# Four layers of graph network on one core: background tiles loaded on another queue, attention ranges in ascending order, entry counts in bf16 pairs

## The chip, the cores and the metric

The kernel runs on one core of a Trainium2 chip, in one launch. The metric is the device time of one execution in microseconds (us); lower is better. "PE" is TensorE, "DVE" VectorE, "ACT" ScalarE, "POOL" GpSimd, and "SP" SyncE, which only issues DMAs here. ACT and POOL issue DMAs too.

## The reference

Inputs are `x` (2708 x 512) and a dense matrix `adj` (2708 x 2708, float32, about 1% of its entries not zero). Each layer ends in a layernorm of (its input plus its output). The constants and unused inputs are left out here:

```python
deg = max(sum(adj != 0, axis=-1), 1)
# layer 0
inc = adj + normalised(adj > 0);  x = layernorm(x + (inc @ x) / sum(inc, -1))
# layer 1
type_sum = adj @ x
attn_a = sigmoid([type_sum, x] @ Wa.T);  attn_b = sigmoid([type_sum, x] @ Wb.T)
h = x @ W_sa;  s_left = h @ a_sa[0, :512];  s_right = h @ a_sa[0, 512:]
e = where(adj != 0, exp(-leaky_relu(s_left[:, None] + s_right[None, :])), 0)
x_a = (e / (sum(e, 1) + 1e-5)) @ h
x_b = adj @ (x @ W_gcnb) + b_gcnb
x = layernorm(x + sigmoid(attn_a * x_a + attn_b * x_b))
# layer 2: three hops
out = x @ W[0];  p = x;  for i in 1..3: p = adj @ p; out += p @ W[i]
x = layernorm(x + out)
# layer 3
a_norm = dinv * (adj + I) * dinv, dinv = rsqrt(deg)
x = layernorm(x + relu((a_norm @ x + x) @ W3 + b3))
```

So `adj`, or a matrix of its shape, is multiplied by a 2708 x 512 matrix seven times, and the count of entries of each row (`deg`) is needed in layer 3 only.

## The kernel before

The host passes `adj` transposed (`adjT`). Rows and columns are cut in two halves of `NH` = 1354, a half has `KT` = 11 tiles (ten of 128 and one of 74; the short rows of both halves are packed into the tiles `r` and `r32`). Every product is done with fewer block products than a plain 2 x 2 blocking, so that DVE makes sums and differences of quarters of `adj` ahead of PE: `sweep` does seven products in place of eight on tiles of `adj` of 128 x (256 to 384) columns; `sweep2` does the same at two levels.

Work is listed by hand. `at(pos, fn)` puts a function into a list with a position, the list is sorted by position and run; each function records its instructions. Each engine keeps its own order of instructions and runs on when its semaphores allow. One unit of position is one block product of one range of columns, so a range takes 7 units. The stages:

- `S[0]`: layer 0, four ranges. `S[1]`: the type sum of layer 1 for the columns 1024 to 1353 of each half only (`RANGES_A`), on which its result (`x_b` times its gate) goes to `XB` in memory; `comb` there also saves the sums of quarters to the memory `SD` (`As` in the profile).
- `S[2]`: attention. Scores `e` are made by ACT (Prelu and Exp, L1142, L1143), DVE masks them by `adj` (L1144), and the sweep multiplies them with `x`. Its ranges are `RANGES_S` = (1024, 330), (768, 256), (384, 384), (0, 384), each with its loads `a<-in_adjT` on SP from one unit ahead of its start. A row of scores `row<-SR` (L1151) is fetched before each.
- Beside `S[2]` runs a *background* pass over the other columns, 0 to 767, in 22 rounds of 1.13 units. A round loads one tile 128 x 512 of each quarter into `bk` (`back_load`, L1058; four tiles with one buffer each), counts its entries (`back_tally`: ACT Sign L1071 and Square L1072, DVE add L1074), makes four sums in place (`back_sums`, DVE L1094) and stores them to `SD` from POOL (L1095). The last round of each half of the columns takes the short rows (`back_rest_load`, L1065) and `back_end` adds the counts up on PE (`ds`, L1102).
- `SB`: the second part of layer 1's type sum, by `sweep2`, on those stored sums. `S[3]` to `S[5]`: the hops. `S[6]`: layer 3.

At the end of each attention range `done2` multiplies with `W_sa` (`dense`, `ps_d`, L611). For the 330 range, which it calls `whole`, everything of layer 1 is then known: it reads `XB` and `X1` on SP, adds (L1201), takes the sigmoid on ACT (L1204), adds `x` (L1167), normalises (statistics L560 to L564 on DVE, the power on POOL L565, L567 on DVE, ACT L570), stores `X2`, transposes it on PE (L600) and stores `X2T`. The other ranges store `x_a` to `XB` (`xa`), and the second part finishes them. `y0_last` reads `X2T` back and multiplies those tiles by a weight of layer 2.

In the type-sum stage `extra1` counts the entries of its columns: one DVE instruction (L976, L979) for each tile of `adj` adds "not zero" into a float32 tile `deg` for each half; `end` adds each up on PE (L993) and `rows` sends the result out by a transpose. Scores of all tiles of `x` are made there as well (L908 on DVE); `score_rows` sends them out by `to_rows`: a PE transpose (L925), an ACT copy (L927) and a store on POOL. The tiles `ld`, `vy`, `sg`, `dg`, `xa`, `y` come from one pool of six buffers (`nat`). In the profile, `acca`, `accu`, `accc`, `accd` are the accumulators of a sweep, `P1c`, `U2`, `W`, `C` its results in SBUF (added up in L524), `run` and `rs` the row sums of `e` (L771, L784), `ps_n` the transposes of L594.

Of the kernel before, what the change touches and what calls it, by code (L numbers as in the profile page):

```python
# [22 lines left out]
BF = mybir.dt.bfloat16  # L23
AF = mybir.ActivationFunctionType
ALU = mybir.AluOpType
P = 128
EPS = 1e-5
NH = 1354
KT = 11
RANGES = [(0, 384), (384, 384), (768, 256), (1024, 330)]  # L30
# [9 lines left out]


RANGES_A = [(1024, 330)]
RANGES_S = [(1024, 330), (768, 256), (384, 384), (0, 384)]
RANGES_B = [(512, 256), (0, 256)]
RANGES2 = [(676, 339), (0, 338)]
EARLY2 = 6
# [4 lines left out]
KW = 2 * K2  # L51
# [3 lines left out]
KR = NH - KW * P  # L55
KA = 2 * KR - 32
# [6 lines left out]
def wt(k):  # L63
    return min(P, NH - k * P) if k < KT else P
# [8 lines left out]
def gnn_kernel(ctx: ExitStack, tc: tile.TileContext, x, adjT, w_sa, a_sa, w_gcn, b_gcn, wab, bab, w_hop, w_out,  # L73
               b_out, out):
    nc = tc.nc
    N, D = x.shape
# [7 lines left out]
    pool = ctx.enter_context(tc.tile_pool(name="pool", bufs=1))  # L84
# [6 lines left out]
    ones_bf = const.tile([P, P], BF, name="ones_bf")  # L91
    nc.vector.memset(ones_bf, 1.0)
    ones_f = const.tile([P, 1], F32, name="ones_f")
# [55 lines left out]
    def move(queue, dst, src):  # L149

        m = dst.shape[0]
        c = m - m % 16 if m > 16 else m
        queue.dma_start(out=dst[:c], in_=src[:c])
        if c < m:
            queue.dma_start(out=dst[c:m], in_=src[c:m])
# [4 lines left out]
    def tmp(nm):  # L160
        return pool.tile([P, 384], F32, name=nm, tag="tmp", bufs=NTMP)
# [18 lines left out]
    def at(pos, fn, hold=False):  # L180

        def go():
            n = len(nc.cur_bb.bb.instructions)
            fn()
            held.update(range(n, len(nc.cur_bb.bb.instructions)))

        events.append((pos, len(events), go if hold else fn))
# [89 lines left out]
    def rows_over(q, t, src):  # L277

        move(q, t[:KR], src[0])
        move(q, t[KR:KA], src[1][: KA - KR])  # L280
# [407 lines left out]
    S = [0.0, 28.0, 35.0, 91.0, 119.0, 147.0, 175.0]  # L688
    SB = 63.0
# [6 lines left out]
    def tiles_of(R0, n):  # L696
        return list(range(R0 // P, (R0 + n + P - 1) // P))
# [189 lines left out]
    deg = {}  # L887
# [42 lines left out]
    def score_rows(R0, h, ts):  # L930
        q = slice(h * KT + ts[0], h * KT + ts[-1] + 1)
        to_rows(s_left[:, q], len(ts), SROW[R0, h])
# [10 lines left out]
    def get_x1(t):  # L943
        got1[t] = fetch(X1[t])

    i = 0
    for R0, n in RANGES:
        full = R0 == RANGES_A[0][0]
        for h in (1, 0):
            ts = tiles_of(R0, n)  # L950
            for k in ts:
                p = S[1] + 0.55 + 0.21 * i
                at(p, lambda t=h * KT + k: get_x1(t))
                at(p + 0.25, lambda t=h * KT + k, w=wt(k), js=range(4 if full else 2): score(t, w, got1, js))
                i += 1
            at(p + 0.26, lambda a=(h * KT + ts[0], len(ts), False): scores_end(*a))
            if full:
                at(p + 0.26, lambda a=(h * KT + ts[0], len(ts), True): scores_end(*a))
            at(p + 0.3, lambda R0=R0, h=h, ts=ts: score_rows(R0, h, ts))
    at(p + 0.27, scores_over)  # L960
    for i, (h, k) in enumerate((h, k) for g in (4, 0) for h in (0, 1) for k in range(g, g + 4)):
        p = S[2] + 1.6 + 1.3 * i
# [5 lines left out]
    def extra1(pb, r, R0, n, A):  # L968
        ts = tiles_of(R0, n)

        def tally(h, key, w=P):

            a = A[(r,) + key]
            if (R0, h) not in deg:
                deg[R0, h] = d = tmp("deg")
                nc.vector.tensor_scalar(d[:w, :n], a[:w, :n], 0.0, None, ALU.not_equal)  # L976
            else:
                d = deg[R0, h]
                nc.vector.scalar_tensor_tensor(d[:w, :n], a[:w, :n], 0.0, d[:w, :n], ALU.not_equal, ALU.add)  # L979

        for ij, p in (("11", -0.6), ("21", 0.05), ("22", 1.05), ("12", 3.6)):
            for k in range(KW):
                at(pb + p + 0.8 * k / KT, lambda ij=ij, k=k: tally(int(ij[0]) - 1, (ij, k)))
        for h, p in ((1, 2.0), (0, 4.5)):
            at(pb + p, lambda h=h: tally(h, ("r", h), KA))
            at(pb + p, lambda h=h: tally(h, ("r32", h), 32))

        def end(h):
            d = deg.pop((R0, h))
            ps = bank("ds", [P, 4])  # L990
            for i, q in enumerate(ts):
                wq = wt(q)
                nc.tensor.matmul(ps[:wq, i : i + 1], d[:, q * P - R0 : q * P - R0 + wq], ones_f, start=True, stop=True)  # L993
            for i, q in enumerate(ts):
                wq = wt(q)
                o = rdeg[:wq, h * KT + q : h * KT + q + 1]
                nc.vector.tensor_scalar(o, ps[:wq, i : i + 1], 1.0, None, ALU.max)
                nc.vector.tensor_scalar(diag[:wq, h, q : q + 1], o, 1.0, None, ALU.add)
                nc.vector.reciprocal(o, o)

        def rows(h):
            to_rows(rdeg[:, h * KT + ts[0] : h * KT + ts[-1] + 1], len(ts),
                    DROW[h][0, ts[0] * P : (ts[-1] + 1) * P].rearrange("(k i) -> k i", i=P))

        at(pb + 2.6, lambda: end(1))
        at(pb + 3.2, lambda: rows(1))
        at(pb + 5.2, lambda: end(0))
        at(pb + 5.8, lambda: rows(0))

    def done1(p0, dp, last, R0, n, h, C, tiles):  # L1010
        Z = {}
# [42 lines left out]
    def back_load(i0, k):  # L1054
        back["t"] = ts = back_tiles()
        for t, (hi, hj) in zip(ts, QUARTERS):
            j0, c0 = hj * NH + k * P, hi * NH + i0
            nc.sync.dma_start(out=t, in_=adjT[j0 : j0 + P, c0 : c0 + D])  # L1058

    def back_rest_load(i0):  # L1060
        back["t"] = ts = back_tiles()
        for h in range(2):
            a = adjT[:, h * NH + i0 : h * NH + i0 + D]
            rows_over(nc.sync, ts[h], (a[NH - KR : NH], a[2 * NH - KR :]))
            nc.sync.dma_start(out=ts[2 + h][:32], in_=a[2 * NH - 32 :])  # L1065

    def tally(pair, w):

# [21 lines left out]
    def back_sums(i0, k):  # L1090
        a11, a21, a22, a12 = back["t"]
        for m, o, a, b, op in (("s1", a22, a21, a22, ALU.add), ("s3", a21, a11, a21, ALU.subtract),
                               ("s2", a11, a22, a11, ALU.subtract), ("s4", a12, a12, a11, ALU.subtract)):
            nc.vector.tensor_tensor(o, a, b, op)  # L1094
            nc.gpsimd.dma_start(out=SD[m][k * P : (k + 1) * P, i0 : i0 + D], in_=o)  # L1095

    def back_end(i0):
        d = back.pop("d")
        ps = bank("ds", [P, 8])
        for h in range(2):  # L1100
            for i in range(4):
                nc.tensor.matmul(ps[:, 4 * h + i : 4 * h + i + 1], d[:, h, i * P : (i + 1) * P], ones_bf[:, 0:1], start=True,  # L1102
                                 stop=True)
        for h in range(2):
            q = slice(h * KT + i0 // P, h * KT + i0 // P + 4)
            o = rdeg[:, q]
            nc.vector.tensor_scalar(o, ps[:, 4 * h : 4 * h + 4], 1.0, None, ALU.max)
            nc.vector.tensor_scalar(diag[:, h, i0 // P : i0 // P + 4], o, 1.0, None, ALU.add)
            nc.vector.reciprocal(o, o)
# [5 lines left out]
    p = S[2] + 1.3  # L1115
    for i0, _ in RANGES_B:
        at(p, back_start)
        for k in range(KW):
            at(p, lambda i0=i0, k=k: back_load(i0, k))
            at(p + 0.4, back_tally)  # L1120
            at(p + 0.55, lambda i0=i0, k=k: back_sums(i0, k))
            p += 1.13
        at(p, lambda i0=i0: back_rest_load(i0))
        at(p + 0.4, back_rest_tally)
        at(p + 0.6, lambda i0=i0: back_end(i0))
        at(p + 0.9, lambda i0=i0: back_rows(i0, 0))
        at(p + 0.95, lambda i0=i0: back_rows(i0, 1))
        p += 1.13
# [93 lines left out]
            at(q + 0.1, d)  # L1222
            at(q + 0.32 + 0.6 * dp * i, e)

    sweep(S[2], RANGES_S, prep=prep2, extra=extra2, done=done2, sums=True)


    def split(h, r0, w):
# [249 lines left out]
    def y0_last(t, w, r0):  # L1478
        g, (i0, m) = next((g, r) for g, r in enumerate(RANGES2) if r[0] <= r0 and r0 + w <= r[0] + 2 * r[1])
        xT = pool.tile([P, DC, P], F32, name="xT", tag="xT", bufs=2)  # L1480
        nc.sync.dma_start(out=xT[:, :, :w], in_=X2T[g, t // KT][:, r0 - i0 : r0 - i0 + w].rearrange("(c p) i -> p c i", p=P))
        y0_rows(xT, w, t)

    for i, (h, k) in enumerate((h, k) for h in (1, 0) for k in tiles_of(*RANGES_A[0])):
        at(SB + 0.9 + 0.8 * i, lambda t=h * KT + k, w=wt(k), r0=k * P: y0_last(t, w, r0))

    def doneB(p0, dp, g, i0, n, h, cc, tiles):
        Z = {}
# [63 lines left out]
    for i in range(4):  # L1552
        for g, p in enumerate((SB + 19.3 + 1.8 * i, S[3] + 6.6 + 1.3 * i)):
            a = ({}, g, i // 2, i % 2)
# [173 lines left out]
    last, done = {}, {}  # L1728
    for n, i in enumerate(list(nc.cur_bb.bb.instructions)):
        p = last if n < 3 * strict else done if n in held else {}  # L1730
# [44 lines left out]
```

## Time and profile before

| what | us |
|---|---|
| median of 3 runs | 2939.11 |
| lowest and highest run | 2936.87, 2945.16 |
| profiled execution | 2952.44 |
| its span | 2950.4 |
| PE busy | 2845.3 (96%) |
| DVE busy | 2297.5 (78%) |
| ACT busy | 635.4 (22%) |
| POOL busy | 597.5 (20%) |

The profile is of one execution on the chip: span is the time from its first to its last instruction. "Busy" leaves out register, semaphore and DMA-issuing instructions. A line such as `PE ps_d L611 <- DVE P1c L524: 11.8, 2, 8.3` in the list of waits says that PE, at line 611, waited for DVE's line 524: 11.8 us in all, twice, 8.3 the longest. In the timeline the bracket after an instruction is the idle time of its engine before it and what ended it. "PEclk" or granted clock is the TensorE clock that was granted, 1 being full speed. The stages in the trace: layer 0 to 437 us, the type sum to 565, attention to 690, 770, 890 and 1010 (its four ranges), the second part to 1370, the hops to 1760, 2140 and 2520, layer 3 to the end.

### The profile page before, as it was taken

To read this page: it belongs to the slowest core of one execution; us is meant where nothing else is said; L and a number is where in the kernel's file an instruction comes from. 1 tells how busy PE (TensorE), PEld (TensorE's weight loads), DVE (VectorE), ACT (ScalarE), POOL (GpSimd) and SP (SyncE) were. 2 spreads that over 40 slices of the span, in tenths; PEclk is the share of its full clock that TensorE was granted. 3 is DMA by queue.
4 is the path that set the end of the run, shared out by engine and by line. 5 is a ranking of instruction groups with operands and counts; after the bars stand their busy time and mean duration, and the time that the engine had idled before them with its cause. 6 is when DMAs were issued, how large, how long until landed. Compare 5 with 4: busy or idle time off the path is not lost.

```text
span 2950.4 us, 38888 instructions
## 1 busy us (share of the span) xinstructions
PE 2845.3 (96%) x11165; PEld 1919.7 (65%) x11165; DVE 2297.5 (78%) x5912; ACT 635.4 (22%) x1255; POOL 597.5 (20%) x1075
## 2 busy tenths in 40 slices
PE   7999998998999999999999999999999999999998
PEld 5655665566756577777666666666666666656664
DVE  6898797686785636667589877988778877899986
ACT  3554200566656410211200000000000100100001
POOL 0133223212211100123202215012240221501102
PEclk9999998999999999999999999999999999999999
DMA  7666466466666445578668668566685566854542
GB/s 224 182 207 182 137 197 198 138 214 182 223 211 193 133 133 154 169 208 249 212 204 245 202 182 271 158 191 211 194 255 165 169 202 185 242 155 142 179 141 78
DMA packets 410238, 554.41 MB, mean 188 GB/s; under 512 B 68656, under 2 KB 350460, under 8 KB 410024
## 3 DMA queue, kind: packets, MB, share of 16 engines
q1 hardware_dynamic: 343360, 413.52, 48.2%
q0 software_dynamic: 48928, 126.64, 12.9%
q10 hardware_dynamic: 17736, 11.76, 1.4%
q8 instruction: 89, 1.46, 0.2%
q14 instruction: 125, 1.02, 0.1%
HBM read 468.02 MB, written 83.65 MB: 187 GB/s over the span
## 4 chain that ended last, share of the span: by engine, by line
PE 70%; DVE 11%; issue 7%; DMA 6%; POOL 3%; SPq 1%; ACT 1%; POOLq 0%; DVEq 0%; ACTq 0%
PE accd L1355 13%; PE accu L1355 12%; PE accc L1355 12%; PE acca L1355 6%; PE ps_d L611 6%; PE accd L463 4%; PE accc L463 3%; PE accu L463 3%; PE accr L1426 3%; PE acca L463 2%; DVE z L1300 1%; PE accr L1430 1%; POOL rstd L565 1%; DMA ld<-X 1%; DVE vy L908 1%
## 5 line engine op out<-in xcount | busy, mean ns | idle before, releaser
L1300 DVE TENSOR_TENSOR z<-z 128x339 f32<-128x339 f32 (+2 forms) x1176 | 537.7, 488 | 25.4 <-PE accu L1355 14.3
L1373 ACT COPY q<-accu 128x339 f32<-128x339 f32 (+2 forms) x105 | 41.6, 429 | 1062.0 <-PE accu L1355 911.9
L1355 PE MATMUL accc<-s,t 128*128 128x339 f32 (+2 forms) x784 | 233.7, 439 | 0.2 <-DVE s L1300 0.2
L1355 PE MATMUL accu<-z,t 128*128 128x339 f32 (+2 forms) x784 | 227.7, 436 | 4.3 <-DVE z L1300 3.0
L1355 PE MATMUL accd<-z,t 128*128 128x339 f32 (+2 forms) x784 | 227.4, 436 | 1.8 <-DVE q L1437 1.4
L1355 PE MATMUL accc<-z,t 128*128 128x339 f32 (+2 forms) x784 | 226.8, 436 | 0.5 <-ACT q L1373 0.5
L565 POOL TENSOR_TENSOR rstd<-rstd,neg_half 128x1 f32<-128x1 f32 (+3 forms) x91 | 60.6, 666 | 720.7 <-DVE rstd L564 466.9
L1355 PEld LDWEIGHTS accu<-z,t 128*128 128x128 f32 x784 | 148.3, 190 | 71.2 <-DVE z L1300 6.2
L1355 PEld LDWEIGHTS accc<-s,t 128*128 128x128 f32 x784 | 146.8, 190 | 71.1 <-issue 10.7
L1355 PEld LDWEIGHTS accd<-z,t 128*128 128x128 f32 x784 | 148.1, 190 | 65.9 <-DVE q L1437 2.3
L1355 PEld LDWEIGHTS accc<-z,t 128*128 128x128 f32 x784 | 148.2, 190 | 64.8 <-ACT q L1373 1.0
L1300 DVE TENSOR_TENSOR s<-z 128x339 f32<-128x339 f32 (+2 forms) x392 | 177.4, 487 | 9.8 <-PE accd L463 3.8
L1379 DVE TENSOR_TENSOR q<-q,accd 128x338 f32<-128x338 f32 (+2 forms) x140 | 67.7, 484 | 146.1 <-PE accd L1355 145.8
L1574 POOL DMA_DIRECT2D Y<-y x192 | 104.6, 552 | 322.4 <-DVE y L1569 289.8
L408 DVE TENSOR_TENSOR a<-a,a 128x384 f32<-128x384 f32 (+2 forms) x240 | 117.8, 511 | 0.7
L1144 DVE SCALAR_TENSOR_TENSOR a<-a,e 128x384 f32<-128x384 f32 (+2 forms) x160 | 77.5, 505 | 51.0 <-ACT e L1143 44.7
L1142 ACT ACTIVATE e<-row,s_right 128x384 f32<-128x384 f32 (+4 forms) x176 | 94.5, 566 | 33.6 <-DMA row<-SR 16.8
L570 ACT ACTIVATE ld<-ld,rstd 128x512 f32<-128x512 f32 (+3 forms) x45 | 36.5, 813 | 256.9 <-DVE rstd L567 94.1
L1095 POOL DMA_DIRECT2D As<-bk x80 | 43.5, 543 | 223.5 <-DVE bk L1094 212.2
L1437 DVE TENSOR_TENSOR q<-q,accr 128x338 f32<-128x338 f32 (+2 forms) x160 | 69.0, 483 | 20.7 <-PE accr L1430 20.5
L1379 DVE TENSOR_TENSOR q<-q,accu 128x338 f32<-128x338 f32 (+2 forms) x175 | 79.0, 483 | 3.8 <-ACT q L1373 2.6
L775 DVE SCALAR_TENSOR_TENSOR s<-a,row 128x384 f32<-128x384 f32 (+2 forms) x152 | 75.0, 506 | 6.0 <-ACT row L760 6.0
(694 smaller groups left out, 5884.1 us busy)
## 6 DMA issues: line engine op xcount, KB each, us to landing
z<-As SPq DMA_DIRECT2D x320, 169.5 KB
z<-As SPq DMA_DIRECT2D x320, 169.0 KB
z<-in_adjT SPq DMA_DIRECT2D x240, 169.5 KB
z<-in_adjT SPq DMA_DIRECT2D x240, 169.0 KB
a<-in_adjT SPq DMA_DIRECT2D x160, 192.0 KB
bk<-in_adjT SPq DMA_DIRECT2D x80, 256.0 KB
As<-bk POOLq DMA_DIRECT2D x80, 256.0 KB, 3.5
z<-As SPq DMA_DIRECT2D x160, 128.0 KB
```

Of the source, the lines that this page charges most:

```text
L408: nc.vector.tensor_tensor(A[r, dst, k][:, :n], A[r, a, k][:, :n], A[r, b, k][:, :n], op)
L463: nc.tensor.matmul(B[home, c][:, :n], X[STAT[p], k][:, c * P : (c + 1) * P], A[r, MOV[p], k][:, :n], start=bool(start and k == k0), stop=k ...
L565: nc.gpsimd.tensor_tensor(rstd[:w, 1:2], rstd[:w, 0:1], neg_half[:w], ALU.pow)
L611: nc.tensor.matmul(o, lhs(c), r, start=c == 0 and n == 0, stop=c == DC - 1, skip_group_check=True)
L775: nc.vector.scalar_tensor_tensor(t[:w, :n], a[:w, :n], 0.0, row[R0, h][:w, :n], ALU.is_gt, ALU.mult)
L1142: nc.scalar.activation(e[:w, :n], row[R0, h][:w, :n], AF.Prelu, bias=s_right[:w, t : t + 1], alpha=0.01)
L1144: nc.vector.scalar_tensor_tensor(a[:w, :n], a[:w, :n], 0.0, e[:w, :n], ALU.not_equal, ALU.mult)
L1300: nc.vector.tensor_tensor(d[:, :n], Z[x + (k,)][:, :n], Z[y + (k,)][:, :n], op)
L1355: nc.tensor.matmul(B[home][:, :n], stat(v, k), a[:, :n], start=bool(start and k == 0), stop=k == nk - 1, skip_group_check=True)
L1379: nc.vector.tensor_tensor(d[:, :n], s_[:, :n], B[home][:, :n], ALU.add)
L1426: nc.tensor.matmul(ps[r][:, :n], XA[:KA, c * P : (c + 1) * P], R[h, s][:KA, :n], start=True, stop=False, skip_group_check=True)
L1574: nc.gpsimd.dma_start(out=rows[:, :, f * P : (f + 1) * P], in_=o[32 * f : 32 * (f + 1), : m * P].rearrange("p (b d) -> p b d", d=P))
```

## The change

Three things are changed, with the positions that go with them. The background tiles are loaded by GpSimd's queue, and their tally, their sums and the end of the count are listed .15 to .25 units later. The attention ranges go in ascending order, so that the 330 range with its full epilogue is the last; `y0_last` is listed later. In the type-sum stage entries are counted as in the background: ACT's Sign and Square of two tiles into one bf16 tile, and one DVE add for both halves; both ends of the count come at 5.2 units. Besides, the rows of scores are sent out .5 units later.

```diff
@@ -40,7 +40,6 @@
 
 
 RANGES_A = [(1024, 330)]
-RANGES_S = [(1024, 330), (768, 256), (384, 384), (0, 384)]
 RANGES_B = [(512, 256), (0, 256)]
 RANGES2 = [(676, 339), (0, 338)]
 EARLY2 = 6
@@ -956,7 +955,7 @@
             at(p + 0.26, lambda a=(h * KT + ts[0], len(ts), False): scores_end(*a))
             if full:
                 at(p + 0.26, lambda a=(h * KT + ts[0], len(ts), True): scores_end(*a))
-            at(p + 0.3, lambda R0=R0, h=h, ts=ts: score_rows(R0, h, ts))
+            at(p + 0.8, lambda R0=R0, h=h, ts=ts: score_rows(R0, h, ts))
     at(p + 0.27, scores_over)
     for i, (h, k) in enumerate((h, k) for g in (4, 0) for h in (0, 1) for k in range(g, g + 4)):
         p = S[2] + 1.6 + 1.3 * i
@@ -968,29 +967,31 @@
     def extra1(pb, r, R0, n, A):
         ts = tiles_of(R0, n)
 
-        def tally(h, key, w=P):
-
-            a = A[(r,) + key]
-            if (R0, h) not in deg:
-                deg[R0, h] = d = tmp("deg")
-                nc.vector.tensor_scalar(d[:w, :n], a[:w, :n], 0.0, None, ALU.not_equal)
+        def pair(keys, w=P):
+            m = pool.tile([P, 2, D], BF, name="sg", tag="nat", bufs=6)
+            for h, key in enumerate(keys):
+                nc.scalar.activation(m[:w, h, :n], A[(r,) + key][:w, :n], AF.Sign)
+            nc.scalar.activation(m[:w, :, :n], m[:w, :, :n], AF.Square)
+            if R0 not in deg:
+                deg[R0] = d = pool.tile([P, 2, D], BF, name="dg", tag="nat", bufs=6)
+                nc.vector.tensor_copy(d[:w, :, :n], m[:w, :, :n])
             else:
-                d = deg[R0, h]
-                nc.vector.scalar_tensor_tensor(d[:w, :n], a[:w, :n], 0.0, d[:w, :n], ALU.not_equal, ALU.add)
-
-        for ij, p in (("11", -0.6), ("21", 0.05), ("22", 1.05), ("12", 3.6)):
-            for k in range(KW):
-                at(pb + p + 0.8 * k / KT, lambda ij=ij, k=k: tally(int(ij[0]) - 1, (ij, k)))
-        for h, p in ((1, 2.0), (0, 4.5)):
-            at(pb + p, lambda h=h: tally(h, ("r", h), KA))
-            at(pb + p, lambda h=h: tally(h, ("r32", h), 32))
+                d = deg[R0]
+                nc.vector.tensor_tensor(d[:w, :, :n], d[:w, :, :n], m[:w, :, :n], ALU.add)
+
+        for k in range(KW):
+            at(pb + 0.1 + 0.8 * k / KT, lambda k=k: pair((("11", k), ("21", k))))
+            at(pb + 3.9 + 0.8 * k / KT, lambda k=k: pair((("12", k), ("22", k))))
+        for key, w in (("r", KA), ("r32", 32)):
+            at(pb + 4.8, lambda key=key, w=w: pair(((key, 0), (key, 1)), w))
 
         def end(h):
-            d = deg.pop((R0, h))
+            d = deg[R0]
             ps = bank("ds", [P, 4])
             for i, q in enumerate(ts):
                 wq = wt(q)
-                nc.tensor.matmul(ps[:wq, i : i + 1], d[:, q * P - R0 : q * P - R0 + wq], ones_f, start=True, stop=True)
+                nc.tensor.matmul(ps[:wq, i : i + 1], d[:, h, q * P - R0 : q * P - R0 + wq], ones_bf[:, 0:1], start=True,
+                                 stop=True)
             for i, q in enumerate(ts):
                 wq = wt(q)
                 o = rdeg[:wq, h * KT + q : h * KT + q + 1]
@@ -1002,10 +1003,10 @@
             to_rows(rdeg[:, h * KT + ts[0] : h * KT + ts[-1] + 1], len(ts),
                     DROW[h][0, ts[0] * P : (ts[-1] + 1) * P].rearrange("(k i) -> k i", i=P))
 
-        at(pb + 2.6, lambda: end(1))
-        at(pb + 3.2, lambda: rows(1))
+        at(pb + 5.2, lambda: end(1))
+        at(pb + 5.9, lambda: rows(1))
         at(pb + 5.2, lambda: end(0))
-        at(pb + 5.8, lambda: rows(0))
+        at(pb + 5.9, lambda: rows(0))
 
     def done1(p0, dp, last, R0, n, h, C, tiles):
         Z = {}
@@ -1055,14 +1056,14 @@
         back["t"] = ts = back_tiles()
         for t, (hi, hj) in zip(ts, QUARTERS):
             j0, c0 = hj * NH + k * P, hi * NH + i0
-            nc.sync.dma_start(out=t, in_=adjT[j0 : j0 + P, c0 : c0 + D])
+            nc.gpsimd.dma_start(out=t, in_=adjT[j0 : j0 + P, c0 : c0 + D])
 
     def back_rest_load(i0):
         back["t"] = ts = back_tiles()
         for h in range(2):
             a = adjT[:, h * NH + i0 : h * NH + i0 + D]
-            rows_over(nc.sync, ts[h], (a[NH - KR : NH], a[2 * NH - KR :]))
-            nc.sync.dma_start(out=ts[2 + h][:32], in_=a[2 * NH - 32 :])
+            rows_over(nc.gpsimd, ts[h], (a[NH - KR : NH], a[2 * NH - KR :]))
+            nc.gpsimd.dma_start(out=ts[2 + h][:32], in_=a[2 * NH - 32 :])
 
     def tally(pair, w):
 
@@ -1117,12 +1118,12 @@
         at(p, back_start)
         for k in range(KW):
             at(p, lambda i0=i0, k=k: back_load(i0, k))
-            at(p + 0.4, back_tally)
-            at(p + 0.55, lambda i0=i0, k=k: back_sums(i0, k))
+            at(p + 0.6, back_tally)
+            at(p + 0.7, lambda i0=i0, k=k: back_sums(i0, k))
             p += 1.13
         at(p, lambda i0=i0: back_rest_load(i0))
-        at(p + 0.4, back_rest_tally)
-        at(p + 0.6, lambda i0=i0: back_end(i0))
+        at(p + 0.6, back_rest_tally)
+        at(p + 0.85, lambda i0=i0: back_end(i0))
         at(p + 0.9, lambda i0=i0: back_rows(i0, 0))
         at(p + 0.95, lambda i0=i0: back_rows(i0, 1))
         p += 1.13
@@ -1222,7 +1223,7 @@
             at(q + 0.1, d)
             at(q + 0.32 + 0.6 * dp * i, e)
 
-    sweep(S[2], RANGES_S, prep=prep2, extra=extra2, done=done2, sums=True)
+    sweep(S[2], RANGES, prep=prep2, extra=extra2, done=done2, sums=True)
 
 
     def split(h, r0, w):
@@ -1482,7 +1483,7 @@
         y0_rows(xT, w, t)
 
     for i, (h, k) in enumerate((h, k) for h in (1, 0) for k in tiles_of(*RANGES_A[0])):
-        at(SB + 0.9 + 0.8 * i, lambda t=h * KT + k, w=wt(k), r0=k * P: y0_last(t, w, r0))
+        at(SB + 2.6 + 0.7 * i, lambda t=h * KT + k, w=wt(k), r0=k * P: y0_last(t, w, r0))
 
     def doneB(p0, dp, g, i0, n, h, cc, tiles):
         Z = {}
```

## The prediction, made before the changed kernel was run

> **What bounds the kernel now.** I read the page's busy line and chain first, then a table of stretches, then the waits of the stretches that the change touches.
>
> ```profile
> PE 2845.3 (96%) x11165; PEld 1919.7 (65%) x11165; DVE 2297.5 (78%) x5912; ACT 635.4 (22%) x1255; POOL 597.5 (20%) x1075
> PE 70%; DVE 11%; issue 7%; DMA 6%; POOL 3%; SPq 1%; ACT 1%; POOLq 0%; DVEq 0%; ACTq 0%
> ```
>
> TensorE (PE) is the bound: 105 of 2950.4 us are not PE work. Only its stalls can be won, or added to. The table (columns: length, busy us and count of PE, weight loads, DVE, ACT, POOL; granted clock; DMA share; GB/s) tells where they are.
>
> ```profile
> 437.00:565.00 128.00, 110.37 (x407) 69.73 (x406) 96.08 (x407) 28.14 (x65) 40.55 (x75) 0.93 0.59 178
> 565.00:690.00 125.00, 112.64 (x428) 74.63 (x426) 88.20 (x243) 88.55 (x164) 20.71 (x35) 0.96 0.62 189
> 690.00:770.00 80.00, 69.13 (x304) 56.70 (x305) 59.31 (x163) 50.26 (x98) 16.14 (x28) 0.93 0.68 205
> 770.00:890.00 120.00, 115.97 (x414) 76.00 (x413) 88.89 (x225) 74.20 (x141) 20.00 (x37) 0.95 0.68 213
> 890.00:1010.00 120.00, 113.53 (x375) 70.93 (x374) 79.18 (x183) 70.14 (x132) 15.07 (x28) 0.94 0.59 184
> 1010.00:1370.00 360.00, 359.82 (x1594) 276.17 (x1593) 225.15 (x603) 49.91 (x93) 52.97 (x92) 1.00 0.57 164
> ```
>
> Row 1 is the type-sum stage, rows 2 to 5 the four attention ranges (330, 256, 384, 384 columns), row 6 the second part of layer 1. All edits but one lie in rows 1 to 5, where PE lacks 51.4 us of 573; row 6 has no idle and full clock. PE's waits from 380 to 1060 us (total, times, longest):
>
> ```profile
> PE ps_d L611 <- DVE P1c L524: 11.8, 2, 8.3
> PE ps_n L594 <- DVE ld L830: 7.7, 1, 7.7
> PE rs L784 <- DVE run L771: 6.9, 2, 4.0
> PE accd L463 <- DVE a L408: 6.3, 6, 3.5
> PE ps_r L925 <- DVE s_left L919: 5.9, 2, 5.2
> PE ps_d L611 <- DVE C L524: 5.8, 1, 5.8
> PE ds L1102 <- DVE dg L1074: 3.0, 1, 3.0
> ```
>
> Each names DVE, but DVE itself waits for ACT or a transfer. So I read SP's queue in the same stretch:
>
> ```profile
> SPq L1058 <- DMA As<-bk: 126.1, 52, 13.2
> ...
> SPq L1151 <- DMA SR<-rows: 16.9, 1, 16.9
> ```
>
> The issue of a background load (L1058) waits until the previous round's store has left its tile, and everything that SP has to issue stands behind it. In the timeline of PE (start, length):
>
> ```profile
> 689.84 1.22 PE L611 MATMUL ps_d<-T1B,P1c 128*128 128x256 f32 x2 [8.33 <-DVE P1c L524]
> ...
> 692.55 1.06 PE L611 MATMUL ps_d<-T2D,P1c 128*128 128x256 f32 x2
> 693.41 0.69 PE L611 MATMUL ps_d<-T3B,U 128*128 128x256 f32 x2
> 693.93 0.59 PE L611 MATMUL ps_d<-T3D,U 128*128 128x256 f32 x2
> 694.36 0.59 PE L611 MATMUL ps_d<-T4B,U 128*128 128x256 f32 x2
> ```
>
> Before this DVE had waited 6.05 us for a tile of the next range, which SP issued late: it stood 10.6 us at `ld<-X` (no free buffer) and then at two background loads. After the stall pairs start .85 us apart for 3.6 us, then .43: 1.8 us more.
>
> **What the Trainium skill says.** (1) "Trainium Kernel Development and Optimization", Key Constraints: queues of SP, ACT and POOL share the same 16 DMA engines; issuing from several saves only sequencer time. The trace agrees: 413.52 MB took 48.2% on SP's queue, 126.64 MB 12.9% on POOL's (.117 and .102% per MB). So the move changes no transfer time, only who stands in line. (2) "DMA: Bandwidth & Descriptors", Anatomy of one DMA — SWDGE (gpsimd) path: about 2.0 us + bytes/436e3, 2.6 us for 256 KB; the 256 KB stores from POOL here took 3.5 us in the median, which I use. (3) "TensorE: Matmul & The Clock Gate", What's actually happening: after an idle window of about 3.4 us the clock halves for as long again. Agrees with the 3.6 us above: a stall over 3.4 us costs 1.8 more. (4) "VectorE: DVE Perf Modes", Side-by-side: 16-bit add, two elements a cycle. Agrees: 1024 bf16 took 685 ns, 512 f32 684.
>
> **The change, part by part** (against the profiled execution, 2952.4 us; the median of the runs is 13.3 less).
>
> *Score rows .5 unit later (unit: a seventh of a range).* The transposes L925 in row 1 get past the sums they wait for: stalls of 5.2 and 1.5 us with 1.8 of half rate, 8.6 at most, and 0 if the next matmul then waits. Row 1's other stalls (ps_n, 7.7 and 2.1) stay. **−6**.
>
> *Entry counts in bf16 pairs.* Out: 42 DVE tallies of 128x330 (40 of .49 us, two of .33): −20 us. In: 22 bf16 adds or copies of 660 elements, 685 × 660/1024 ≈ .44, 10 us. DVE −10, of 96 busy. ACT gets 44 Signs of 330 (.47 us, as L718's mask) and 22 Squares of 660 (between .62 and 1.04, say .75): +37 on its 28 of 128. Both `ds` groups now stand together before the gate matmuls, behind ACT's last pairs; what waits behind them is all of PE. PE's six f32 column sums become bf16: nothing. PE isn't waiting for the tallies now, so DVE's relief hides beside PE; −2 if ld L830 comes sooner, +5 if `ds` waits. **0**.
>
> *Ascending ranges.* Out: the stall at 690 (8.3 + 1.8), since the 330 range's epilogue no longer holds `ld<-X` ahead of the 256 range's loads: −10. SP's 16.9 us for the score rows go too, at no PE time. In: this epilogue (dense L611, L1201, sigmoid L1204, layernorm with POOL's power L565, scale L570, transposes L600) now ends the stage. In the built order PE has some 7 us of accumulation between the first dense result and the third transpose. Chain for the first tile of h=0, by the durations of these lines before: L1201 .75, table load 1.28 and sigmoid .63, add L1167 .69, statistics .69, .17 and .14, power with its way there and back 1.1, L567 .16, scale .81, in sum 6.4 us. The two further tiles add about 3 each (three DVE passes of .7 and the scale), and the eight weight loads (L1462) that ACT issues in between some 3 (8 × .37): ≈ 15; less 7 = 8, and 1 at h=1, where two more products stand behind it. **+9**, 4 if these overlap, 33 to 43 in the rival below. Net −1. The dense product from stored rows (y0_last) moves 1.7 units later behind the later store; row 6 has no wait there now: 0.
>
> *Background loads on POOL, use later.* 80 loads of 256 KB and 20 pieces leave SP, so its 126.1 + 14.0 us of waits (L1058, L1065) go; nothing of range loads stands behind them. They stand on POOL instead: each load waits for a store of the same round, up to two landings of 3.5 us × 20 rounds = 140 us, plus 100 issues × .54 = 54. POOL has 72 busy of 445 (rows 2–5): room, but the powers L565 and XB stores queue behind, 3.5 to 7 us each; DVE and ACT wait for powers only in the epilogue. Tallies listed .2 unit later give loads 3.4 us in a long range (17 us a unit), 2.3 in the 256 one; ACT's 20 waits for bk are 54.0 us in all, 2.7 on average, longest 8.1. So in the long ranges the stalls behind these go: 633 (4.0, rs), 867 (2.9, rs), 925 (3.5, ps_d), 998 (3.0, ds), 13.4 us. In the 256 range a round comes every 1.13 × 80/7 = 12.9 us while rounds ran 13.8, 11.8 and 15.8 us apart (DVE's first sums at 725.9, 739.7, 751.5, 767.3): its stalls 729 (3.5), 761 (1.2), 769 (5.8) stay, 10.5. **−13**; at most −31 with these and 7 of half rate, at least 0.
>
> Sum: −6 + 0 − 1 − 13 = **−20**: 2932 in a profiled execution, **2919** at the median.
>
> **Rivals.**
> *The boundary stalls (slower).* Before, the same epilogue took from the first dense result to the last scale 20.2 us (h=0, 695.2 to 715.4) and 27 (h=1, 647.8 to 674.9), because POOL and SP were busy with background. If it does at 1010 too, PE lacks 13 after its 7 us, 11.5 at h=1 after 15.5, two half rates 3.6, SP held by `ld<-X` 10 as at 659, next combs late 5: 43. Against gains of 29 (6, 10, 13): **+14, 2953**. It decides from a boundary of 29 us on. For: one buffer pool of six serves `ld`, `y`, `sg`. Against: the background is at its end there.
> *Waits change queue only (no change).* POOL's waits delay loads as SP's did, the stalls stay; boundary 15: −6 − 10 + 15 = **−1, 2938**. For: the single buffer per tile remains and bounds a round. Against: SP's range loads are freed in any case.
> *All background stalls go (faster still).* −8.6 − 10 + 4 − 31 ≈ **−46, 2893**. Against: the 256 range's period.
>
> **How the numbers follow.** Forecast .42 (its own ends 2905 to 2931), more .10, none .16, slower .32. Faster by over 0.3% (8.8 us, about what a measurement of this kernel can tell from no change): .42 + .10 = .52; same .16; slower .32. The range goes from the best case, 2893, to the slower one plus 11 for its own spread, 2964: what lies beyond is perhaps .15.
>
> **What would show it.** Right: no SP wait at L1058; no stall at ps_r in the type sum; 330 range last with ps_n or accu waiting 5 to 15 us near its end; rs and ds stalls under 1 us in 384 ranges; 256 range as before. Wrong: PE busy in 437–1010 not above 522; POOL waits for As over 200 us with `rstd` waiting behind; `ds` waiting for ACT; a boundary of 29 us or more.

## The result, and the profile after

The changed kernel takes 2929.39 us (median of 12 runs, 2923.41 to 2936.50), the kernel before 2940.89 us (12 runs): ratio 0.9957, 95% interval 0.9945 to 0.9968, so 12.6 us less by the ratio. The two profiled executions, 2952.44 and 2930.68 us, differ by more, because the one of before lay 11.5 us above its median; 4.4 us of their difference lie before any changed line (the first matmul of the second range of layer 0 starts at 128.4 and at 124.0 us).

The busy line and the chain, from the page of the changed kernel:

```profile
PE 2832.2 (97%) x11159; PEld 1913.9 (65%) x11159; DVE 2292.8 (78%) x5890; ACT 661.3 (23%) x1314; POOL 650.8 (22%) x1175
PE 71%; DVE 12%; issue 6%; DMA 6%; POOL 3%; ACT 1%; SPq 1%; POOLq 0%; DVEq 0%; ACTq 0%
```

PE is still the bound. ACT's busy time rises with the Signs and Squares. POOL's rises with the moved issues: an issue by POOL counts as busy in these traces (.54 us each, 100 more of them), unlike one by SP or ACT. The same stretches of time as before:

```profile
437.00:565.00 128.00, 117.40 (x430) 73.03 (x431) 96.50 (x399) 66.45 (x135) 34.91 (x65) 0.95 0.57 175
565.00:690.00 125.00, 120.72 (x409) 73.95 (x408) 91.33 (x219) 79.65 (x144) 29.12 (x53) 0.99 0.63 194
690.00:770.00 80.00, 74.03 (x238) 44.83 (x237) 58.69 (x137) 50.12 (x94) 19.73 (x37) 0.96 0.59 187
770.00:890.00 120.00, 110.51 (x478) 87.01 (x477) 78.37 (x236) 69.39 (x148) 39.39 (x74) 0.96 0.63 193
890.00:1010.00 120.00, 105.16 (x422) 76.19 (x421) 83.20 (x212) 62.76 (x120) 31.96 (x60) 0.93 0.60 183
1010.00:1370.00 360.00, 359.81 (x1624) 279.23 (x1623) 242.59 (x646) 59.97 (x111) 65.78 (x111) 1.00 0.63 186
```

PE is busy 527.8 of the 573 us of the first five rows, before 521.6. The gain is in the first three rows; rows four and five are worse than before (110.5 and 105.2 against 116.0 and 113.5). The rows are the same times, not the same ranges. By the first sweep matmul of each, the attention ranges began at 563.9, 679.6, 793.7 and 918.7 us before, and the second part at 1051.9; so the 256 range took 114 us, not the 80 of row three. In the changed kernel the ranges (384, 384, 256, 330) begin at 552.4, 679.6, 809.1 and 905.8 us and the second part at 1029.3. PE's waits from 380 to 1060 us in the changed kernel:

```profile
PE rs L783 <- DVE run L770: 21.1, 4, 8.7
PE ds L1103 <- DVE dg L1075: 6.7, 1, 6.7
PE ps_d L610 <- ACT sg L1073: 6.0, 1, 6.0
PE ps_r L924 <- DVE s_left L918: 4.8, 2, 4.5
PE ps_n L593 <- DVE P1c L523: 3.7, 1, 3.7
PE ps_r L924 <- DVE s_right L919: 2.1, 1, 2.1
```

The waits for `ld` (7.7), for the sums `P1c` and `C` ahead of `ps_d` (11.8 and 5.8) and for `a` at `accd` (6.3) are no longer in the list. The waits that come from the background have grown: `rs` from 6.9 to 21.1 us, `ds` from 3.0 to 6.7, and a dense product (of `P1c`, at 914 us) waits 6.0 us, by its releaser for the background's Square. Neither `ps_r` nor `rs` did what was forecast. SP's and POOL's queues in the same stretch, two lines of each:

```profile
SPq L398 <- DVE a L1145: 113.5, 35, 13.0
SPq L398 <- PE accc L462: 67.8, 22, 16.0
```

```profile
POOL As L1096 <- DVE bk L1095: 147.4, 50, 14.7
POOL bk L1059 <- DMA As<-bk: 65.1, 38, 4.7
```

SP no longer waits for stores of the background. Instead it waits for free buffers of the ranges' tiles: 113.5 us for DVE's mask, where 34.4 were. So most of its 126 us had been waiting time with nothing else to do. POOL now waits 65.1 us for stores before loads.

A table that the rest leans on is read from each kernel's trace. The two stages are timed from first to first sweep matmul. For the attention stage there follow PE's idle time (its gaps of over .7 us) and the time for which it worked while the granted clock was one half. The last column is the median time of a background load from its issue to the last of the 16 increments of its semaphore. Each row is one execution.

| kernel | type sum, us | attention, us | PE idle, us | PE at half clock, us | load of a background tile, us |
|---|---|---|---|---|---|
| before | 126.4 | 488.0 | 33.1 | 40.6 | 3.71 (SP) |
| changed | 118.2 | 476.9 | 34.6 | 23.5 | 4.56 (POOL) |
| only score rows later | 123.0 | 482.2 | 33.1 | 31.2 | |
| only pairs | 118.5 | 485.2 | 35.1 | 32.1 | |
| only ascending ranges | 129.2 | 457.5 | 18.9 | 17.1 | 3.56 (SP) |
| only background | 123.2 | 492.6 | 40.6 | 35.7 | 4.56 (POOL) |
| changed, background undone | 119.2 | 457.1 | 17.6 | 18.0 | 3.52 (SP) |

Work at half clock takes twice its time (in the lines of the prediction, pairs of matmuls start .85 us apart and then .43), so half of that column is lost. Idle time and this loss together leave 434.6 us of the attention stage before, and 430.1 to 434.2 in the other rows: the kernels differ there in little else.

From the 785th matmul of L1355 (L1356 after), which starts at 1330.5 us before, to the end every kernel run here takes 1616.6 to 1624.0 us, the kernel before 1619.9 and the changed one 1619.8. The changes don't reach beyond it.

### The profile page after: what moved, and what is told of

It reads as the page before. It is cut to its first block, busy times and chain, and to the rows that moved or that the text cites. A ratio compares the mean times of both kernels' runs of the same rounds, so it can differ in the third digit from the quotient of the medians.

```text
span 2928.9 us, 38864 instructions
## 1 busy us (share of the span) xinstructions
PE 2832.2 (97%) x11159; PEld 1913.9 (65%) x11159; DVE 2292.8 (78%) x5890; ACT 661.3 (23%) x1314; POOL 650.8 (22%) x1175
## 4 chain that ended last, share of the span: by engine, by line
PE 71%; DVE 12%; issue 6%; DMA 6%; POOL 3%; ACT 1%; SPq 1%; POOLq 0%; DVEq 0%; ACTq 0%
PE accd L1356 13%; PE accu L1356 13%; PE accc L1356 12%; PE ps_d L610 6%; PE acca L1356 6%; PE accd L462 4%; PE accc L462 3%; PE accr L1427 3%; PE accu L462 3%; DMA bk<-in_adjT 2%; PE acca L462 2%; DVE z L1301 2%; DMA As<-bk 1%; PE accr L1431 1%; PE ps L649 1%
## 5 line engine op out<-in xcount | busy, mean ns | idle before, releaser
L1356 PE MATMUL accc<-s,t 128*128 128x339 f32 (+2 forms) x784 | 233.5, 439 | 0.2 <-DVE s L1301 0.2
L1356 PE MATMUL accu<-z,t 128*128 128x339 f32 (+2 forms) x784 | 227.7, 436 | 4.2 <-DVE z L1301 3.0
L1356 PE MATMUL accd<-z,t 128*128 128x339 f32 (+2 forms) x784 | 227.8, 436 | 1.7 <-DVE q L1438 1.4
L1356 PE MATMUL accc<-z,t 128*128 128x339 f32 (+2 forms) x784 | 226.8, 436 | 0.5 <-ACT q L1374 0.5
L1356 PEld LDWEIGHTS accu<-z,t 128*128 128x128 f32 x784 | 148.1, 190 | 70.1 <-DVE z L1301 6.1
L1356 PEld LDWEIGHTS accc<-s,t 128*128 128x128 f32 x784 | 146.8, 190 | 70.7 <-issue 10.2
L1356 PEld LDWEIGHTS accd<-z,t 128*128 128x128 f32 x784 | 148.1, 190 | 66.7 <-DVE q L1438 2.3
L1356 PEld LDWEIGHTS accc<-z,t 128*128 128x128 f32 x784 | 148.2, 190 | 64.8 <-ACT q L1374 1.0
L1143 ACT ACTIVATE e<-row,s_right 128x384 f32<-128x384 f32 (+5 forms) x176 | 94.8, 566 | 41.0 <-DVE a L1145 11.6
L1144 ACT ACTIVATE e<-e 128x384 f32<-128x384 f32 (+5 forms) x176 | 78.9, 475 | 1.4
```

The source lines that it names most:

```text
L1143: nc.scalar.activation(e[:w, :n], row[R0, h][:w, :n], AF.Prelu, bias=s_right[:w, t : t + 1], alpha=0.01)
L1144: nc.scalar.activation(e[:w, :n], e[:w, :n], AF.Exp, scale=-1.0)
L1356: nc.tensor.matmul(B[home][:, :n], stat(v, k), a[:, :n], start=bool(start and k == 0), stop=k == nk - 1, skip_group_check=True)
```

## The experiments

Each ratio is to the kernel before, with its 95% interval; a gain in us is the ratio times 2940.

**1. Only the score rows later.** `at(p + 0.3, ... score_rows)` to `p + 0.8` (`p + 0.4` for the last row, whose range comes first).

> The kernel before with only the rows of scores listed .5 units later (the last one, columns 1024 of half 0, by .1, since its row is fetched soon after). By the prediction's first step the stalls of PE at ps_r in the type-sum stage (5.2 and 1.5 us and 1.8 of half rate) go: about -6 us, 2935. Rival: the transposes only come past one wait for DVE, and the next matmul waits for the same DVE: within 2 us of before, with a stall of 4 to 5 us left at ps_r or at the next line.

Measured: 2937.73 us, ratio 0.9998 (0.9988 to 1.0008). Three of PE's waits from 380 to 1060 us there:

```profile
PE ps_n L594 <- DVE ld L830: 6.1, 1, 6.1
PE pg L1017 <- DVE C L524: 2.4, 1, 2.4
PE ps_r L925 <- DVE s_left L919: 2.1, 2, 1.8
```

At `ps_r` 5.9 us have become 2.1, but the gate matmuls `pg`, which did not wait before, wait 2.4 us. In the kernels that leave this stage alone its length is 123.2 to 129.2 us; 123.0 is no clear gain, and the whole time shows none. The rival holds: most of what was won at `ps_r` (3.8 us) comes back as a wait for DVE at the next line that needs it (2.4).

**2. Only the pairs.** `extra1` of the changed kernel in the kernel before.

> The kernel before with only the entry counts in bf16 pairs. By the prediction 0 us: DVE busy in the type sum falls by about 10 of 96, ACT rises by 37, PE's stalls there stay (ps_n 7.7, 2.1; ps_r 5.2, 1.5). Rival 1: DVE's relief reaches PE, since its first waits in that stage all name DVE: -4 us, ps_n 7.7 falls to 4 (3.7 in the changed kernel). Rival 2: PE waits for ACT's tallies at ds before the gate matmuls: +5 us.

Measured: 2933.33 us, ratio 0.9987 (0.9979 to 0.9994), 3.8 us less. The first rival holds:

```profile
PE ps_r L925 <- DVE s_left L919: 8.4, 5, 4.0
PE ps_n L594 <- DVE ld L830: 3.1, 1, 3.1
PE ps_n L594 <- DVE P1c L524: 1.2, 1, 1.2
```

The first waits of the stage, 7.7 and 2.1 before, are 3.1 and 1.2; PE doesn't wait at this stage's `ds`. The stage takes 118.5 us.

**3. Only the ascending ranges** (and `y0_last` later).

> The kernel before with only the attention ranges in ascending order and the dense product from stored rows listed later. The trace of the changed kernel shows no PE stall from 985 to 1060 us, so the boundary should cost 0 to 2 here too, and the stall at 690 (8.3 and 1.8 of half rate) goes: -8 to -10 us, 2931 to 2933. By the prediction's own number (boundary +9) -1. Rival: the SP queue still holds the background loads, and the same kind of stall comes at another boundary of ranges: 0, with a ps_d stall of over 5 us at one of them.

Measured: 2913.88 us, ratio 0.9924 (0.9910 to 0.9938): 22.3 us less (4 runs), more than the whole change and more than any theory gave. All waits of 3 us and more that are left in PE's list from 380 to 1060 us:

```profile
PE ps_n L594 <- DVE ld L830: 8.0, 1, 8.0
PE rs L784 <- DVE run L771: 6.2, 1, 6.2
PE ds L1102 <- DVE dg L1074: 5.8, 1, 5.8
PE ps_r L925 <- DVE s_left L919: 4.2, 2, 3.5
PE ps_d L611 <- DVE C L524: 3.9, 1, 3.9
PE ps_r L925 <- DVE s_right L920: 3.3, 2, 3.0
PE ps_d L611 <- DVE P1c L524: 3.0, 1, 3.0
```

`ps_d` for `P1c` is 3.0 where 11.8 were, and `accd` for `a` (6.3 before) is not among them. Idle gaps of PE of over .7 us in the attention stage sum to 18.9 us, before to 33.1. Not only the stall at 690 went. The whole stage, before and here:

```profile
563.90:1051.90 488.00, 454.26 (x1679) 306.17 (x1678) 328.30 (x845) 285.22 (x536) 77.28 (x138) 0.95 0.60 184
559.50:1017.00 457.50, 438.62 (x1667) 299.31 (x1666) 320.53 (x827) 271.84 (x521) 72.00 (x131) 0.98 0.62 192
```

PE is also busy 15.6 us less, for the same matmuls but for 12 transposes (1.1 us) that now come later: the granted clock is .98 where it was .95. Fewer stalls bring fewer spells of half clock (three of 20.5 us in all, before seven of 47.8). Time idle explains 14 of the 30.5 us between these two traces, and half clock 12 (half of 40.6 less 17.1). `y0_last` is not the source: from the start of the second part to its 785th matmul it is 279.7 us here, before 278.5.

**4. Only the background on POOL, its use later.** `nc.sync` to `nc.gpsimd` in `back_load` and `back_rest_load`, and the four positions.

> The kernel before with only the background loads on POOL's queue and their use listed later. By the prediction -13 us, the stalls behind the background in the long ranges (4.0, 2.9, 3.5, 3.0) gone. Rival: the waits only change their queue (in the changed kernel PE's waits at rs are 21.1 us where 6.9 were, and at ds 6.7 where 3.0 were): within 3 us of before, or slower by up to 8; SP's 126 us at the background loads gone all the same.

Measured: 2942.84 us, ratio 1.0017 (1.0005 to 1.0029): 5 us more. The rival holds:

```profile
PE rs L784 <- DVE run L771: 15.6, 3, 6.1
PE ps_d L611 <- DVE C L524: 11.2, 3, 6.9
PE ps_d L611 <- DVE P1c L524: 5.1, 2, 4.3
PE ds L1102 <- DVE dg L1074: 4.8, 2, 2.5
```

One forecast wait did shrink: `ps_d` for `P1c`, 11.8 to 5.1, since SP issues the next range's tiles sooner (the 16th and 17th tiles of the 256 range 21 and 8.5 us ahead of its first matmul; before 9.1 ahead and 1.0 after). The others, 6.9 at `rs`, 5.8 at `ps_d` for `C` and 3.0 at `ds`, have grown to 15.6, 11.2 and 4.8.

**5. The changed kernel with the background part undone, and with each half of it undone.** First all of it:

> The changed kernel with the whole background part undone: loads on SP's queue again and the use of the tiles at its old positions (score rows, pairs and ascending ranges stay). Theory: the background part costs time here, and more than it did alone (+5, since the part with ascending ranges has less idle of PE to hide it): 2929 less 12 to 18 = 2911 to 2917, the attention stage 457 us as with ascending ranges alone against 477. Rival (the prediction's -13): without it 2938 to 2942.

Measured: 2910.93 us, ratio 0.9902 (0.9886 to 0.9919). It beats both kernels; beside ascending ranges the background part costs 16 us (28.8 less 12.6). Then only the queue (`nc.gpsimd` back to `nc.sync`):

> The changed kernel with the background loads on SP's queue again, their use still listed later. If the queue is what costs, as POOL's order puts each load behind a store of its round (POOL waits 65 us for As in the changed kernel): 2911 to 2917. Rival: the later use costs, since a tile is given back later and the next round's load starts later: within 3 us of the changed kernel's 2929.

Measured: 2913.79 us, ratio 0.9913 (0.9897 to 0.9929). And only the positions:

> The changed kernel with the use of the background tiles at its old positions, loads still on POOL's queue. If the queue costs: within 4 us of 2929, or slower, since ACT and DVE now wait longer for bk. Rival (the later use costs): 2911 to 2917.

Measured: 2926.36 us, ratio 0.9955 (0.9940 to 0.9971). It is the queue: with SP's the gain is doubled, wherever the use is listed, and the positions alone are worth nothing that these runs show. ACT's wait for the tiles from 540 to 1060 us, first with the background undone, then changed:

```profile
ACT sg L1072 <- DMA bk<-in_adjT: 39.8, 26, 5.1
```

```profile
ACT sg L1072 <- DMA bk<-in_adjT: 70.0, 25, 8.6
```

From the first store of a round to the landing of the next round's fourth load it is 11.7 us (median) with SP and 13.4 with POOL: a load lands 1.0 us later after its issue; the rest is put down to standing behind stores in one queue, which was not measured by itself. ACT keeps its order, DVE waits for it and PE for DVE: by the lists of waits `bk` late makes Sign late, then the sums, then `run` and `rs`.

**6. Two of the four loads on POOL.** The changed kernel with the background part undone, and in `back_load`:

```diff
-        for t, (hi, hj) in zip(ts, QUARTERS):
+        for t, (hi, hj), q in zip(ts, QUARTERS, (nc.sync, nc.gpsimd, nc.gpsimd, nc.sync)):
...
-            nc.sync.dma_start(out=t, in_=adjT[j0 : j0 + P, c0 : c0 + D])
+            q.dma_start(out=t, in_=adjT[j0 : j0 + P, c0 : c0 + D])
```

> The changed kernel with the background part undone, except that two of the four tiles of each round (the two whose stores leave first, so that their loads have slack) are loaded from POOL's queue. A load from POOL lands 4.5 us after its issue, one from SP 3.5 (medians in the traces). If the chain of a round is what costs (last store, load of that tile, count, sums), these two have an issue of slack: 2909 to 2915, no more than 4 above 2911. If each load on POOL's queue costs its share, by occupying the queue or by its slower transfer: about half of the 16 us, 2917 to 2921.

Measured: 2911.32 us, ratio 0.9915 (0.9901 to 0.9929). These 40 loads on POOL, which have slack, cost nothing that can be told; the last landing of a round comes 12.2 us (median) after the first store of the one before. This speaks for the chain of a round, and against a cost for each load on POOL. How the 16 us divide between the slower landing and the standing in line was not separated; nor was a second buffer for each tile, which should take the wait for the store out of the chain, tried.

**7. Which part of the order.** The kernel before with `RANGES_S` in two other orders: 330, 384, 384, 256, and 384, 256, 384, 330.

> The kernel before with the attention ranges in the order 330, 384, 384, 256: only the 256 range is moved, to the end; the 330 range with its full epilogue stays first, amid the background. Theory (the gain of ascending ranges is the epilogue leaving the background): within 3 us of before, 2935 to 2941, with a ps_d stall of 6 to 9 us left after the first range. Rival 1 (the gain is that the 256 range, in which the background's rounds come every 12.9 us, stands later and runs shorter): 2918 to 2926. Rival 2: slower by up to 5, if the last range then has too little time for the rest of the background before the second part.

> The kernel before with the attention ranges in the order 384, 256, 384, 330: against ascending order the 256 range is second instead of third; the 330 range with its epilogue is last. If the two halves of the gain (epilogue out of the background; 256 range later) stand alone: -9 to -13 us, 2926 to 2930, with the stalls of the 256 range back (3.5, 1.2 and 5.8 us before). If only the epilogue matters and the run with it first gained by something else: 2913 to 2917.

Measured: 2926.90 us, ratio 0.9956 (0.9940 to 0.9972), and 2914.44 us, ratio 0.9931 (0.9915 to 0.9947). The second is as good as ascending order: with the epilogue at the end, the 256 range does no harm in second place. So it was not by its shortness alone that this range stalled. With the epilogue first and a 384 range after it, half of the gain comes, although the stall after the first range stays (gaps of PE in the attention stage: 27.8 us here, 18.2 with 384, 256, 384, 330):

```profile
PE rs L784 <- DVE run L771: 10.0, 2, 6.1
PE ps_d L611 <- DVE P1c L524: 8.3, 1, 8.3
```

The length of each range, from its first sweep matmul to that of the next, with its columns:

| kernel | first, us | second, us | third, us | fourth, us |
|---|---|---|---|---|
| before | 115.7 (330) | 114.1 (256) | 125.0 (384) | 133.2 (384) |
| 330, 384, 384, 256 | 115.7 (330) | 143.8 (384) | 124.5 (384) | 91.6 (256) |
| 384, 256, 384, 330 | 125.7 (384) | 94.8 (256) | 123.9 (384) | 109.9 (330) |
| only ascending ranges | 127.7 (384) | 120.1 (384) | 93.5 (256) | 116.1 (330) |

What costs in the kernel before is the epilogue of the 330 range beside the background, and it falls into the range behind it: 256 columns take 114.1 us there and 91.6 to 94.8 elsewhere, 384 columns take 143.8 there and 120.1 to 133.2 elsewhere. A longer range in that place is not seen to hide more of it. My expectation for the first run (no gain) was right on that stall and wrong on the whole: its gain lies in the third and fourth range. They take 42.1 us less than before, where a 256 range in place of a 384 one is worth 26.6 (120.1 less 93.5). Why they run better was not tested.

**8. The changed kernel with the old order.**

> The changed kernel with the attention ranges in the old, descending order and the dense product from stored rows at its old place (the last row of scores comes .4 units earlier, as its range is fetched first). If the parts simply add up (pairs -4, background +5 by their runs alone): 2939 to 2943. If the background part costs as much as it does beside ascending ranges (+15 to +18): 2950 to 2956.

Measured: 2938.34 us, ratio 1.0003 (0.9995 to 1.0011): close to the plain sum. So the background part costs about 5 with the old order and 16 with the new. A reading would be that SP's freedom pays some of it back at the stall after the 330 range (`ps_d` for `P1c`, 11.8 before, 5.1 in experiment 4 and 5.4 here). But the 256 range, in which that stall lies, is not shorter: 118.5 and 115.1 us, before 114.1. Why the cost is smaller with the old order stays open.

**9. Sums on PE later still.** The changed kernel with the background undone, `score_rows` at `p + 1.5`, `back_end` at `p + 1.0` and the rows that it sends out just behind it.

> The changed kernel with the background part undone, and with two sums on PE listed later still: score rows 1.5 units after their scores instead of .8, and the end of each background count .4 units later. It had PE stalls of 5.3 and 1.4 us at ps_r and 4.5 at ds. If a sum of columns listed behind what it waits for lets PE go on: -6 to -9 us against the kernel with only the background undone (2911), 2902 to 2905. Rival (as with the score rows alone, which gained nothing): the wait comes back at the next line that needs DVE, within 3 us of 2911.

Measured: 2914.29 us, ratio 0.9929 (0.9914 to 0.9944). There is no gain, and the rival holds again (the kernel with only the background undone took 2911). The waits of 5.3 and 1.4 us at `ps_r` for scores and 4.5 at `ds` L1103 are .3 and none, and in PE's list stand

```profile
PE ds L993 <- DVE dg L980: 11.3, 1, 11.3
PE ps_r L924 <- DVE diag L1109: 6.2, 1, 6.2
```

which were 2.1 and none.

## Why the prediction was right or wrong

The number was near: 2919 forecast, 2929 measured, and faster by over 0.3% as the likeliest case had it. Its steps were not, so that was luck: one part gained what another was to gain, and a cost beside it took back half. By the runs of one part alone:

| step | forecast, us | alone, us | what failed |
|---|---|---|---|
| score rows | −6 | −0.6 | the end it gave itself, 0 "if the next matmul then waits", was the truth |
| pairs | 0 | −3.8 | DVE's relief was said to hide beside PE |
| ascending order | −1 | −22.3 | both terms |
| background | −13 | +5.0 | sign |
| sum | −20 | −21.7 | the change: −12.6 |

*Ascending order, the cost.* "PE has some 7 us of accumulation between the first dense result and the third transpose" left out the dense products of the other two tiles, which stand there as well. From the changed kernel's timeline of PE (start, length), lines left out between:

```profile
1033.65 0.59 PE L610 MATMUL ps_d<-T4D,U 128*128 128x256 f32 x2
...
1034.94 0.59 PE L610 MATMUL ps_d<-T1B,P1c 128*128 128x256 f32 x2
...
1039.26 0.59 PE L610 MATMUL ps_d<-T1B,P1c 128*74 128x256 f32 x2
...
1044.01 2.32 PE L1356 MATMUL accd<-z,t 128*128 128x256 f32 x10
1046.16 0.60 PE L599 MATMUL ps_t<-ident,ld 128*128 128x128 f32 x4
...
1048.77 0.41 PE L599 MATMUL ps_t<-ident,ld 74*128 74x74 f32 x3
```

The first dense result is there at 1034.2, the third transpose starts at 1048.8, 14.5 us later and without a bracket of idle time. The chain was sized well (15 us forecast; the scale of the third tile ends at 1048.7, so there is nothing to spare); the cover was twice what was counted, so the cost is 0, not 9. The slower rival priced the boundary by epilogues of before that had the background beside them; at 1030 there is none (PE's sum of its last count starts at 985).

*Ascending order, the gain.* Only the stall that followed the epilogue at once was credited to it (8.3 us, and 1.8 of half rate). The term that was mis-sized most is the half rate. The prediction gave 1.8 us to a stall of over 3.4 us and nothing to a shorter one. By the clock records of the kernel before, half clock lasted until 9.3 us after the 3.0 us stall that ended at 998, and until 6.9 us after the 2.9 us stall that ended at 867. In the attention stage it lost 20.3 us that way before and 8.6 with ascending ranges alone (half of 40.6 and of 17.1), so some 12 of the 30.5 us between these two traces are there. Idle time, 33.1 to 18.9, is another 14. The 256 range alone had 18.9 of it and keeps 6.2.

The 10.5 us of stalls in the 256 range that were to "stay" mostly did: with 384, 256, 384, 330, where that range has the background but no epilogue beside it, they are 7.8 (1.1 at `accd`, none at `ps_d`, 6.7 at `rs`). But their reason, a round every 12.9 us, rests on a range of 80 us; by its sweep matmuls the range took 114, which makes 18.4 us a round.

*Background.* "The move changes no transfer time, only who stands in line": here a POOL load landed after 4.6 us and an SP load after 3.5. The Trainium skill, "Trainium Kernel Development and Optimization", Key Constraints, says that the queues of SP, ACT and POOL all run on the same 16 DMA engines. The bytes' share agrees, but the latency is another thing, and for a chain of single buffers latency is part of the price. "Tallies listed .2 unit later give loads 3.4 us": the later listing alone was worth nothing (experiment 5). That SP's waits go was right, and worth little at PE: SP then waited for the buffers of the ranges' tiles (113.5 us). The rival "waits change queue only" had this mechanism, with the single buffer per tile that bounds a round; it did not see that the round would become longer.

*Pairs.* The work was sized well: DVE's tallies took 21.3 us before and its adds 10.8 after. All of the stage's waits named DVE, and that relief did come through. ACT's added work (28.1 to 66.5 us busy in row one) cost nothing, as forecast.

The parts don't add up: −21.7 alone against −12.6 together. Experiments 4, 5 and 8 show where it is: the background part costs 5 with the old order and 16 with the new.

## What to carry to other kernels

A queue's waiting time is worth what its engine would do next; look what it would wait for then, before crediting it. Where a tile has one buffer, the time of a round is store, load and work in series, so the queue with the shorter landing time belongs there; loads with slack could go elsewhere here at no cost. Put a long epilogue where no other side work runs, and count everything that PE has between its first result and its last use as cover. Price a stall with the half clock that follows it, read from the clock records. Don't credit a wait of PE for DVE that is only listed later: here it came back at the next line.

## What the runs showed of the hardware

A load of 256 KB from HBM to SBUF landed 3.5 us (median of 80; two kernels) after its issue from SP's queue and 4.6 us (median of 80; the changed kernel) after its issue from POOL's. One of the two kernels with SP differs from the changed one in the queue alone. POOL was occupied .54 us by each issue, SP .33 us, which can be .2 of the difference. The slowest of the 80 took 5.1 and 5.4 us from SP and 7.2 from POOL.

In the attention stage of the kernel before, the granted clock was either full or one half. The half came in seven spells of 3.4, 6.8 or 10.2 us, 47.8 us in all, and two of them went with stalls of PE of only 2.9 and 3.0 us.
